# Two attention layers on one core: products cut in two and spread between the pieces of the heads, the first q by weight rows, the token sums' pool ahead of the prologue

## The chip, the cores and the metric

The kernel runs on one core of one Trainium2 chip. The metric is the device time of one execution in microseconds (us). Of the kernel before three runs are shown: 2143.07, 2144.46 and 2144.91 us; the median is 2144.46 us. One execution was also profiled; every view of a profile below is of that one execution.

Five engines work side by side, each through its own list of instructions: PE (TensorE, matrix products and transposes, with its weight loads shown apart as PEld), DVE (VectorE), ACT (ScalarE), POOL (GpSimd) and SP (SyncE, which here only issues DMAs). They wait for one another by semaphores.

## The reference

Two cross-attention layers, one after the other, over the same context. All arrays are float32. There are B = 8 batches, S = 100 queries, C = 640 channels in H = 20 heads of D = 32. The context has 77 text tokens, then 645 image tokens, of 1024 channels each.

```python
# layer 0 (x: 8 x 100 x 640; text = context[:, :77], ip = context[:, 77:])
q = x @ Wq.T
out = attend(q, text @ Wk.T, text @ Wv.T) + attend(q, ip @ Wk_ip.T, ip @ Wv_ip.T)
x1 = out @ Wo.T + bo + x
# layer 1, of x1, with weights of its own
q = x1 @ Wq
text_out = attend(q, text @ Wk, text @ Wv)
text_probs = softmax((q @ k_text.T) / sqrt(32))            # over all 640 channels
sem = ((text_probs @ text) @ ip.T) / sqrt(32)
ip_probs = softmax(scores_ip + 0.5 * sem) * mask           # mask: one number a query
out = (text_out + ip_probs @ v_ip) @ Wout + bout + x1
```

`attend` works head by head: softmax(q k / sqrt(32)) v. By far the most arithmetic is in the keys and values of the image tokens, 645 tokens by 1024 channels into 2 × 640 columns for each of 8 batches and 2 layers.

## The kernel before

**Units and steps.** A unit u is one batch in one layer: 16 of them (u = 8·layer + batch). Each is done in five steps p, one for each four heads (128 channels), so there are 80 steps n = 5u + p. The loop at the end (line 999 on) writes TensorE's order out by hand: `tc.manual_schedule` keeps PE in the order of the program text, and the other engines' orders are chosen by a scheduler and then fixed. One step holds

- `scores(u, p, 0)`: 4 matmuls of q by the first 512 keys into `sc` (line 782), then on DVE and ACT the row maxima and exponentials (lines 788 to 807);
- `transposes` of the step before, two tiles at a time, six in all (`pspt`, line 838): each is copied out of its bank into `pt` by DVE (line 845), every third by ACT (line 843);
- `scores(u, p, 1)`, the remaining 133 + 77 keys, and after it the small chain that joins the two parts (lines 811 to 828), with the last scaling of the probabilities on ACT (line 822) and DVE (lines 823 and 826);
- `values` of the step before (`pv`, line 860): probabilities by values, copied out by DVE (line 864).

**What fills the gaps.** Between those parts stand four calls `between(n, a, b, small)` (line 983). `small` holds the step's pieces: of a finished group of units the output projection in five pieces `out_piece` (`pso`, line 708, evicted by DVE with bias and residual at line 713), for layer 1 the next q in five pieces `q_piece` (`psq`, line 727, evicted by ACT at line 731), and three parts of `sem` (`psm`, lines 667 to 691). The rest is the production of keys and values for later units: `production()` (line 873) makes one list `todo` of tasks, each with a cost in us and a due step that `spread` works out so that each step gets about as much PE work as the others. `make(until)` runs the tasks that are due. After the pieces of a call one more task is taken ahead of its due time, when none was made in the call.

**Production.** Units 0 to 13 are made in pairs (`pair_tasks`, line 424), in five blocks of 128 tokens (133 in the last). A block begins with `begin`: it loads the next block's x, and has `token_sums` (line 182) form four sums of quarters of x on DVE and POOL. Then come `last_k` (`psk4`, line 453: 8 matmuls of 256 columns, for the last 128 key channels), for layer 1 two products of text by image (`psg`, line 465), and two series of seven products for the values (`psv`, line 475) and the other keys (`psk`, line 483): Strassen's scheme, in which the products of the series read the sums of x or of the weights. Product 1 (`psk_a`) reads x itself; the next, `psk_b`, is the first that needs a token sum. Units 14 and 15 are made singly (`single_tasks` and `last_tasks`), by `plain_product` (line 540, with its matmuls at line 544): 8 matmuls into one bank, then a copy.

**Memory.** [...] In the steps `sc` takes four, `ps_pt` two, which transposes, values and all pieces share in turn, and `ps_pj` two, for the products.

**The prologue** (lines 192 to 353) makes q of layer 0 and the text's keys and values of both layers. The first q: for each of five channel blocks c and two halves g of the batches, five matmuls over the rows k of Wq with 400 columns (4 batches), then an ACT copy (line 228) and stores by POOL (line 230). On SP the first loads are half of x, the five blocks of Wq, the other half of x, then the text and the text weights. `load_left` (line 311) loads eight weight blocks `wl` for the five image tokens beyond 640 (`left_v`, stored to `vl_d`). The prologue's memory, pool `first`, is given back at its end, and the pools of the steps, `sums` for the token sums among them (line 358), are laid out after that, over it.

Of the kernel before, what the change touches and what calls it, by code (L numbers as in the profile page):

```python
# [9 lines left out]
F32 = mybir.dt.float32  # L10
AF = mybir.ActivationFunctionType
# [3 lines left out]
P = 128  # L15
B = 8
# [27 lines left out]
def two_layer_xattn(  # L44
# [22 lines left out]
    cpool = ctx.enter_context(tc.tile_pool(name="ctx", bufs=2))  # L67
    dram = ctx.enter_context(tc.tile_pool(name="scratch", bufs=1, space=bass.MemoryType.DRAM))
# [61 lines left out]
    def product_ps(name):  # L130
        return pj[0].tile([P, 512], F32, tag="pj", name=name)
# [60 lines left out]
    with ExitStack() as es:  # L192
# [4 lines left out]
        nc.sync.dma_start(xt[:, :4], x_t[:, :4])  # L197
        for k in range(NC_):
            t = fp.tile([P, C], F32, tag="wq", name=f"wq0_{k}", bufs=NC_)
            nc.sync.dma_start(t, wq[0][k * P : (k + 1) * P, :])  # L200
            wq0.append(t)
        nc.sync.dma_start(xt[:, 4:], x_t[:, 4:])
# [13 lines left out]
        for c in range(NC_):  # L216
            t = fp.tile([P, B * S], F32, tag="q", name=f"q0_{c}", bufs=2)
            for g in range(2):
                ps = product_ps(f"psq_{c}_{g}")
                for k in range(NC_):  # L220
                    nc.tensor.matmul(
                        ps[:, : 4 * S],
                        lhsT=wq0[k][:, c * P : (c + 1) * P],
                        rhs=xt[:, 4 * g : 4 * g + 4, k, :],
                        start=(k == 0),
                        stop=(k == NC_ - 1),
                    )
                nc.scalar.activation(t[:, 4 * g * S : 4 * (g + 1) * S], ps[:, : 4 * S], AF.Copy, scale=SCALE)
            for g in range(B // 2):
                nc.gpsimd.dma_start(  # L230
                    q_d[0][g][:, :, c, :], t[:, 2 * g * S : 2 * (g + 1) * S].rearrange("p (b s) -> p b s", s=S)
                )

# [77 lines left out]
        def load_left(l):  # L311
            for k in range(NCC):
                wl[l, k] = fp.tile([P, C], F32, tag="wl", name=f"wl_{l}_{k}", bufs=NCC)
                nc.sync.dma_start(wl[l, k], wvi[l][k * P : (k + 1) * P, :])
# [43 lines left out]
    spool = ctx.enter_context(tc.tile_pool(name="sums", bufs=1))  # L358
# [65 lines left out]
    def pair_tasks(us):  # L424
# [12 lines left out]
        for j, (n0, n1) in enumerate(BLOCKS):  # L437
# [15 lines left out]
            def last_k(j=j, n=n, ko=ko):  # L453
                ps = product_ps(f"psk4_{us[0]}_{j}")
                for k in range(NCC):
                    nc.tensor.matmul(  # L456
                        ps[:, : 2 * n], lhsT=W["k", 4][:, k, :], rhs=xs[j][:, :, k, :n],
                        start=(k == 0), stop=(k == NCC - 1),
                    )
                nc.scalar.copy(ko[0][:, :, 4, :n], ps[:, : 2 * n].rearrange("p (i n) -> p i n", i=2))  # L460
# [52 lines left out]
            tasks.append((3.6, last_k))  # L513
# [26 lines left out]
    def plain_product(dst, n, lhs, rhs, name):  # L540
        ps = product_ps(name)
        m = dst.shape[0]
        for k in range(NCC):
            nc.tensor.matmul(ps[:m, :n], lhsT=lhs(k), rhs=rhs(k), start=(k == 0), stop=(k == NCC - 1))  # L544
        nc.scalar.copy(dst, ps[:m, :n])

    def wk_plain(c):
        def w(k):
            if c == 4:
                return W["k", 4][:, k]  # L550
            return W["k", f"b{k // HK + 1}{c // 2 + 1}"][:, k % HK, c % 2 * P : (c % 2 + 1) * P]

        return w

    def single_tasks(u):
        tasks, xs, text = [], {}, {}

        def begin():
            b = u % B
            for m in range(3):  # L560
                xs[m] = big_block(u, m)
            text[0] = one.tile([P, NCC, 2 * NT], F32, tag="textt", name=f"textt_{u}")
            nc.sync.dma_start(text[0][:, :, :NT], text_t.rearrange("k p n -> p k n")[:, :, b * NT : (b + 1) * NT])

        def k_one(c, m):
            n0, n1 = BIG[m]
            t = opool.tile([P, 256], F32, tag="ko", name=f"ko1_{u}_{c}_{m}")
            plain_product(t[:, : n1 - n0], n1 - n0, wk_plain(c), lambda k: xs[m][:, k, : n1 - n0], f"psk1_{u}_{c}_{m}")
            nc.gpsimd.dma_start(k_d[u][:, c, n0:n1], t[:, : n1 - n0])

        def v_one(j, h):
            t = opool.tile([P, HC], F32, tag="vo", name=f"vo1_{u}_{j}_{h}")
            at = j % 2 * P
            plain_product(
                t, HC, lambda k: xs[j // 2][:, k, at : at + P],
                lambda k: W["v", f"b{k // HK + 1}{h + 1}"][:, k % HK], f"psv1_{u}_{j}_{h}",
            )
            nc.gpsimd.dma_start(v_d[u][j * P : (j + 1) * P, h * HC : (h + 1) * HC], t)

        def text_one(m):  # L580
            n0, n1 = BIG[m]
            t = one.tile([NT, 2 * NX], F32, tag="gst", name=f"gst_{u}_{m}", bufs=2)
            plain_product(
                t[:, : n1 - n0], n1 - n0, lambda k: text[0][:, k, :NT], lambda k: xs[m][:, k, : n1 - n0],
                f"psg_{u}_{m}",
            )
            nc.gpsimd.dma_start(g_d[u % B][:, n0:n1], t[:, : n1 - n0])

        tasks.append((0.0, begin))
        for m in range(3):  # L590
            n = BIG[m][1] - BIG[m][0]
            tasks += [(0.0137 * n, lambda c=c, m=m: k_one(c, m)) for c in range(NC_)]
            tasks.append((0.0137 * n, lambda m=m: text_one(m)))
            tasks += [(4.3, lambda j=j, h=h: v_one(j, h)) for j in range(2 * m, min(2 * m + 2, NB)) for h in range(2)]
        return tasks

# [3 lines left out]
    def last_tasks():  # L600
# [17 lines left out]
        def text_one(m):  # L618
            n0, n1 = BIG[m]
            t = one.tile([NT, 2 * NX], F32, tag="gst", name=f"gst_{u}_{m}", bufs=2)  # L620
            plain_product(
                t[:, : n1 - n0], n1 - n0, lambda k: text[0][:, k, :NT], lambda k: xs[m][:, k, : n1 - n0],
                f"psg_{u}_{m}",
            )
            nc.gpsimd.dma_start(g_d[b][:, n0:n1], t[:, : n1 - n0])

        def k_one(c, m):
            n0, n1 = BIG[m]
            n = n1 - n0
            if c < 3:  # L630
                dst = opool.tile([P, 256], F32, tag="ko", name=f"ko1_{u}_{c}_{m}")[:, :n]
            else:
                if m == 0:
                    load_k(u, c)
                dst = ks[u, c][:, n0:n1]
            plain_product(dst, n, wk_plain(c), lambda k: xs[m][:, k, :n], f"psk1_{u}_{c}_{m}")
            if c < 3:
                nc.gpsimd.dma_start(k_d[u][:, c, n0:n1], dst)

        def v_one(c, j):  # L640
            if c < 3:
                dst = opool.tile([P, P], F32, tag="vo", name=f"vo1_{u}_{c}_{j}")
            else:
                if j == 0:
                    vs[u, c] = vpool.tile([P, NB, P], F32, tag="v", name=f"v_{u}_{c}")
                dst = vs[u, c][:, j, :]
            at = j % 2 * P
            plain_product(
                dst, P, lambda k: xs[j // 2][:, k, at : at + P], lambda k: wv[c][:, k // 2, k % 2], f"psv1_{u}_{c}_{j}"
            )  # L650
            if c < 3:
                nc.gpsimd.dma_start(v_d[u][j * P : (j + 1) * P, c * P : (c + 1) * P], dst)

        n = [b - a for a, b in BIG]
        return (
            [(0.0, begin)] + [(0.0137 * n[m], lambda m=m: text_one(m)) for m in range(3)],
            [[(0.0137 * n[m], lambda c=c, m=m: k_one(c, m)) for m in range(3)] for c in range(NC_)],
            [[(1.8, lambda c=c, j=j: v_one(c, j)) for j in range(NB)] for c in range(NC_)],
# [310 lines left out]
    with tc.manual_schedule(engines={mybir.EngineType.PE}):  # L969
# [8 lines left out]
        def make(until):  # L978
            while done[0] < len(todo) and todo[done[0]][1] < until:
                todo[done[0]][2]()  # L980
                done[0] += 1

        def between(n, a, b, small):


            before = done[0]
            for i, (_, f) in enumerate(small):
                make(n + a + (b - a) * (i + 1) / (len(small) + 1))
                f()
            make(n + b)  # L990
            while done[0] < len(todo) and todo[done[0]][1] < n + b + 0.4 and not any(
                t for t, _, _ in todo[before : done[0]]
            ):
                todo[done[0]][2]()
                done[0] += 1

# [85 lines left out]
```

## Time and profile before

| | |
|---|---|
| median of the runs shown | 2144.46 us |
| the profiled execution's own time | 2140.97 us |
| its span, first to last instruction | 2139.2 us |
| mean granted TensorE clock | 0.999 |
| PE busy | 2091.2 us (98%), 16670 instructions |
| PEld busy | 1677.7 us (78%) |
| DVE busy | 934.0 us (44%) |
| ACT busy | 864.5 us (40%) |
| POOL busy | 344.2 us (16%) |
| DMA | 241.99 MB, mean 113 GB/s |

The span is taken by the profiler, from the first to the last instruction; the execution's own time has some 2 us around it. A float32 matmul stands in the profile as two instructions ("passes"), each with a weight load of its own, so a product of 8 matmuls is "x16". Matmuls are pipelined: the next starts before one ends, so the pace is read from start to start and not from the length of one. A wait is put down to the instruction that ended it; "issue" means that the profile shows nothing that ended it.

### The profile page before, as it was taken

What the parts mean: (1) busy time and instruction counts of PE and PEld (TensorE: products, weight loads), DVE (VectorE), ACT (ScalarE), POOL (GpSimd) and SP (SyncE); (2) the same over time, 40 slices, a digit from 0 to 9 for tenths busy, and PEclk for the clock granted to TensorE, in tenths of its full rate; (3) what the DMA queues carried; (4) which work ended last, traced back from release to release, by engine and by line L of the source; (5) the groups of instructions that cost most, each with busy time, mean ns of one, the idle gap of its engine ahead of it and who ended that gap; (6) DMA issues with size and microseconds to landing.
All of it is one profiled execution on the core that took longest, in us unless ns stands there. A gap on an engine that the chain in (4) does not pass through costs nothing. (4 is left out here: it accounts for less than half of the span.)

```text
span 2139.2 us, 41528 instructions
## 1 busy us (share of the span) xinstructions
PE 2091.2 (98%) x16670; PEld 1677.7 (78%) x16670; DVE 934.0 (44%) x2380; ACT 864.5 (40%) x2859; POOL 344.2 (16%) x398
## 2 busy tenths in 40 slices
PE   8999999999999999999999999999999999999998
PEld 5676888787788887878878888887777887777887
DVE  1112122455454454454544444444444444454554
ACT  1001000345444444444344444444434445566665
POOL 5214112111010110102401111111111111111110
PEclk9999999999999999999999999999999999999999
DMA  9344223224234333535433333533333354334320
GB/s 344 106 134 163 79 78 102 85 78 124 77 113 136 95 104 104 150 90 165 120 116 114 110 100 93 154 85 99 83 113 99 95 158 128 119 96 122 106 81 7
DMA packets 264974, 241.99 MB, mean 113 GB/s; under 512 B 31466, under 2 KB 233722, under 8 KB 264782
## 3 DMA queue, kind: packets, MB, share of 16 engines
q1 hardware_dynamic: 245022, 171.97, 28.9%
q0 software_dynamic: 19760, 67.38, 9.4%
q8 instruction: 131, 2.15, 0.4%
q14 instruction: 61, 0.50, 0.1%
HBM read 171.68 MB, written 67.61 MB: 112 GB/s over the span
## 5 line engine op out<-in xcount | busy, mean ns | idle before, releaser
L845 DVE COPY pt<-pspt 128x400 f32<-128x400 f32 x320 | 175.6, 568 | 199.3 <-PE pspt L838 172.0
L799 ACT ACTIVATE p<-p,st 100x512 f32<-100x512 f32 (+1 forms) x320 | 176.4, 553 | 135.3 <-DVE st L795 135.3
L799 ACT ACTIVATE p<-sc,st 100x512 f32<-100x512 f32 (+1 forms) x320 | 165.2, 530 | 144.8 <-DVE st L788 144.3
L822 ACT ACTIVATE p<-p,st 100x512 f32<-100x512 f32 x320 | 204.8, 711 | 41.2 <-DVE st L818 39.6
L838 PE MATMUL pspt<-ident,p 100*128 100x100 f32 (+1 forms) x1920 | 209.0, 250 | 8.9 <-DVE pt L845 3.8
L838 PEld LDWEIGHTS pspt<-ident,p 100*128 100x128 f32 (+1 forms) x1920 | 186.5, 137 | 34.5 <-DVE res L713 5.8
L475 PE MATMUL psv_a<-wv,x 128*128 128x320 f32 x560 | 164.6, 437 | 1.5 <-ACT gst L470 1.3
L843 ACT COPY pt<-pspt 128x400 f32<-128x400 f32 (+1 forms) x160 | 78.2, 488 | 213.2 <-PE pspt L838 212.1
L475 PE MATMUL psv_d<-wv,s 128*128 128x320 f32 x560 | 163.5, 435 | 0.0
L795 DVE CUSTOM_DVE_ANT_0 p<-sc,sem 100x512 f32<-100x512 f32 (+1 forms) x320 | 138.8, 490 | 29.1 <-PE sc L782 29.1
L483 PEld LDWEIGHTS psk_a<-x,wk 128*128 128x128 f32 x1120 | 134.3, 193 | 11.9 <-DVE hs L864 3.9
L498 POOL DMA_DIRECT2D v_d<-vo x70 | 39.3, 561 | 632.1 <-DVE vo L172 471.9
L483 PE MATMUL psk_a<-x,wk 128*128 128x128 f32 (+1 forms) x1120 | 139.9, 278 | 1.0 <-ACT ko L148 1.0
L475 PEld LDWEIGHTS psv_a<-wv,x 128*128 128x128 f32 x560 | 102.9, 190 | 47.6 <-issue 5.7
L475 PEld LDWEIGHTS psv_d<-wv,s 128*128 128x128 f32 x560 | 104.4, 190 | 45.5 <-issue 3.1
L483 PE MATMUL psk_d<-s,wk 128*128 128x128 f32 (+1 forms) x1120 | 139.8, 278 | 0.0
L483 PEld LDWEIGHTS psk_d<-s,wk 128*128 128x128 f32 x1120 | 131.1, 191 | 10.2 <-issue 5.5
L782 PE MATMUL sc<-k,q 32*100 32x210 f32 (+1 forms) x1280 | 138.5, 502 | 0.3 <-ACT p L807 0.3
L788 DVE TENSOR_REDUCE st<-sc 100x4 f32<-100x2048 f32 x80 | 120.1, 1501 | 31.9 <-PE sc L782 31.8
L456 PE MATMUL psk<-x,wk 128*128 128x256 f32 (+1 forms) x560 | 128.5, 381 | 1.0 <-ACT vl L329 1.0
L510 POOL DMA_DIRECT2D k_d<-ko x70 | 58.5, 835 | 402.1 <-DVE ko L172 369.4
L456 PEld LDWEIGHTS psk<-x,wk 128*128 128x128 f32 x560 | 102.8, 188 | 18.8 <-DVE s L183 1.6
(177 smaller groups left out, 3393.0 us busy)
## 6 DMA issues: line engine op xcount, KB each, us to landing
x<-ip_t SPq DMA_DIRECT2D x56, 512.0 KB
k<-k_d SPq DMA_DIRECT2D x78, 322.5 KB
v<-v_d SPq DMA_DIRECT2D x78, 320.0 KB
v_d<-vo POOLq DMA_DIRECT2D x70, 320.0 KB, 2.5
k_d<-ko POOLq DMA_DIRECT2D x56, 320.0 KB, 6.8
o<-wo SPq DMA_DIRECT2D x40, 320.0 KB
x<-ip_t SPq DMA_DIRECT2D x16, 532.0 KB
q<-wq SPq DMA_DIRECT2D x20, 320.0 KB
```

The costliest lines, as they stand in the source:

```text
L456: nc.tensor.matmul(ps[:, : 2 * n], lhsT=W["k", 4][:, k, :], rhs=xs[j][:, :, k, :n], start=(k == 0), stop=(k == NCC - 1),)
L475: nc.tensor.matmul(ps[:, :HC], lhsT=sums[which][:, k, :P], rhs=W["v", WHICH[which]][:, k, :], start=(k == 0 and not go_on), stop=(k == HK ...
L483: nc.tensor.matmul(ps[:, r * n : (r + 1) * n], lhsT=W["k", WHICH[which]][:, k, r * P : (r + 1) * P], rhs=sums[which][:, k, :], start=(r == ...
L510: nc.gpsimd.dma_start(k_d[u][:, :, n0 : n0 + n], ko[0][:, h, :, :n])
L782: nc.tensor.matmul(sc[:S, i, : k1 - k0], lhsT=qs_[u][rows, c, :], rhs=ks[u, c][rows, k0:k1], start=True, stop=True)
L788: nc.vector.tensor_reduce(st[:, part, :], sc[:S, :, :n], AX.X, ALU.max, negate=True)
L795: nc.vector.tensor_tensor_reduce(out=img, in0=sc[:S, i, :n], in1=sems[u][:, k0 : k0 + n], scale=-1.0, scalar=3.0e38, op0=ALU.add, op1=ALU. ...
L799: nc.scalar.activation(p[:, i, k0 : k0 + n], img, AF.Exp, bias=st[:, part, i : i + 1], scale=sign, accum_out=st[:, 3 + part, i : i + 1],)
L822: nc.scalar.activation(p[:, i, :KA], p[:, i, :KA], AF.Copy, scale=mul[:, 0, i : i + 1])
L838: nc.tensor.transpose(ps[:rows, i * S : (i + 1) * S], pr[u, c][:, i, j * P : j * P + rows], ident[:S, :S])
L843: nc.scalar.copy(dst, src)
L845: nc.vector.tensor_copy(dst, src)
```

## The change

Four edits.

**The first q** goes through the batches in four pairs g. For each pair three banks are open at once, and the rows k of Wq are outermost: each row block meets all five channel blocks c before the next row is needed, with 200 columns (2 batches) a matmul. The loads of x are four instead of two, one a pair, the first of them ahead of Wq. A pair's q is stored by one DMA. Wq's five blocks and the eight `wl` blocks share one set of eight buffers, `wr`.

**The pool `sums`** is opened ahead of the prologue, so that it has memory of its own.

**Longer products in two tasks.** `last_k` is two tasks of 1.8 us, with the bank held from the first to the second. `plain_product` returns tasks, two halves where its cost is over 2.5 us.

**A product ahead of each piece.** `between` has a helper `apart`: before each piece of `small`, when no product was made since the last mark, tasks are taken from `todo` until one product is among them, as far as 0.4 step beyond the end of the call.

The function `text_one`, twice in the text before, stands once.

```diff
@@ pools
     cpool = ctx.enter_context(tc.tile_pool(name="ctx", bufs=2))
+    spool = ctx.enter_context(tc.tile_pool(name="sums", bufs=1))
     dram = ctx.enter_context(tc.tile_pool(name="scratch", bufs=1, space=bass.MemoryType.DRAM))
...
-    spool = ctx.enter_context(tc.tile_pool(name="sums", bufs=1))
     opool = ctx.enter_context(tc.tile_pool(name="made", bufs=2))
@@ the first q
-        nc.sync.dma_start(xt[:, :4], x_t[:, :4])
+        nc.sync.dma_start(xt[:, :2], x_t[:, :2])
         for k in range(NC_):
-            t = fp.tile([P, C], F32, tag="wq", name=f"wq0_{k}", bufs=NC_)
+            t = fp.tile([P, C], F32, tag="wr", name=f"wq0_{k}", bufs=NCC)
             nc.sync.dma_start(t, wq[0][k * P : (k + 1) * P, :])
             wq0.append(t)
-        nc.sync.dma_start(xt[:, 4:], x_t[:, 4:])
+        for g in range(1, B // 2):
+            nc.sync.dma_start(xt[:, 2 * g : 2 * g + 2], x_t[:, 2 * g : 2 * g + 2])
...
-        for c in range(NC_):
-            t = fp.tile([P, B * S], F32, tag="q", name=f"q0_{c}", bufs=2)
-            for g in range(2):
-                ps = product_ps(f"psq_{c}_{g}")
-                for k in range(NC_):
+        for g in range(B // 2):
+            t = fp.tile([P, 2, NC_, S], F32, tag="q", name=f"q0_{g}", bufs=2)
+            ps = [product_ps(f"psq_{g}_{i}") for i in range(3)]
+            for k in range(NC_):
+                for c in range(NC_):
+                    at = c % 2 * 2 * S
                     nc.tensor.matmul(
-                        ps[:, : 4 * S],
-                        lhsT=wq0[k][:, c * P : (c + 1) * P],
-                        rhs=xt[:, 4 * g : 4 * g + 4, k, :],
-                        start=(k == 0),
-                        stop=(k == NC_ - 1),
+                        ps[c // 2][:, at : at + 2 * S], lhsT=wq0[k][:, c * P : (c + 1) * P],
+                        rhs=xt[:, 2 * g : 2 * g + 2, k, :],
+                        start=(k == 0 and c % 2 == 0), stop=(k == NC_ - 1), skip_group_check=True,
                     )
...
+            nc.gpsimd.dma_start(q_d[0][g], t)
...
-                wl[l, k] = fp.tile([P, C], F32, tag="wl", name=f"wl_{l}_{k}", bufs=NCC)
+                wl[l, k] = fp.tile([P, C], F32, tag="wr", name=f"wl_{l}_{k}", bufs=NCC)
@@ longer products
-            def last_k(j=j, n=n, ko=ko):
-                ps = product_ps(f"psk4_{us[0]}_{j}")
-                for k in range(NCC):
+            def last_k(half, j=j, n=n, ko=ko, open_={}):
+                if half == 0:
+                    open_[j] = product_ps(f"psk4_{us[0]}_{j}")
+                ps = open_[j]
+                for k in range(HK * half, HK * (half + 1)):
...
-            tasks.append((3.6, last_k))
+            tasks += [(1.8, lambda h=h, f=last_k: f(h)) for h in range(2)]
...
-    def plain_product(dst, n, lhs, rhs, name):
-        ps = product_ps(name)
-        m = dst.shape[0]
-        for k in range(NCC):
-            nc.tensor.matmul(ps[:m, :n], lhsT=lhs(k), rhs=rhs(k), start=(k == 0), stop=(k == NCC - 1))
-        nc.scalar.copy(dst, ps[:m, :n])
+    def plain_product(time, make_dst, n, lhs, rhs, name, then=None):
+
+        parts = 2 if time > 2.5 else 1
+        open_ = {}
+
+        def part(i):
+            if i == 0:
+                open_["dst"], open_["ps"] = make_dst(), product_ps(name)
+            dst, ps = open_["dst"], open_["ps"]
+            m = dst.shape[0]
+            for k in range(NCC // parts * i, NCC // parts * (i + 1)):
+                nc.tensor.matmul(ps[:m, :n], lhsT=lhs(k), rhs=rhs(k), start=(k == 0), stop=(k == NCC - 1))
+            if i == parts - 1:
+                nc.scalar.copy(dst, ps[:m, :n])
+                if then:
+                    then(dst)
+
+        return [(time / parts, lambda i=i: part(i)) for i in range(parts)]
@@ a product ahead of each piece
+        mark = [0]
+
+        def apart(until):
+
+            while done[0] < len(todo) and todo[done[0]][1] < until and not any(
+                t for t, _, _ in todo[mark[0] : done[0]]
+            ):
+                todo[done[0]][2]()
+                done[0] += 1
+            mark[0] = done[0]
+
         def between(n, a, b, small):
-
-
-            before = done[0]
+
+            mark[0] = done[0]
             for i, (_, f) in enumerate(small):
                 make(n + a + (b - a) * (i + 1) / (len(small) + 1))
+                apart(n + b + 0.4)
                 f()
             make(n + b)
-            while done[0] < len(todo) and todo[done[0]][1] < n + b + 0.4 and not any(
-                t for t, _, _ in todo[before : done[0]]
-            ):
-                todo[done[0]][2]()
-                done[0] += 1
+            apart(n + b + 0.4)
```

## Prediction

> **What bounds the kernel.** I read the page's first two parts, then busy time by stretches, then TensorE's (PE's) waits, then the timeline where the longest ones fall. The stretches are the prologue with the first pair of images, the heads with enough products beside them, and the last heads with few products left:
>
> ```profile
> core 0: us, PE busy (x) PEld busy (x) DVE busy (x) ACT busy (x) POOL busy (x), PEclk, DMA share, GB/s
> 0.00:385.00 385.00, 373.79 (x1796) 275.68 (x1797) 80.49 (x121) 30.90 (x71) 102.04 (x99) 1.00 0.46 142
> 385.00:1730.00 1345.00, 1331.22 (x11226) 1090.08 (x11225) 652.56 (x1534) 596.06 (x1986) 197.87 (x223) 1.00 0.38 109
> 1730.00:2139.20 409.20, 386.15 (x3651) 311.90 (x3649) 200.96 (x725) 237.49 (x802) 44.34 (x77) 1.00 0.35 101
> ```
>
> TensorE is the bound, DVE and ACT at most six tenths busy. Idle TensorE is 385 − 373.79 = 11.2 us, then 13.8 us, then 23.05 us in the last 409 us alone: 48 of the 2139.2 us. No instruction of TensorE is removed by the change, so only these 48 us and losses of pace can be won. Who ended them (total, times, longest, all in us):
>
> ```profile
> PE psq L221 <- DMA wq<-wq: 6.9, 1, 6.9
> PE pso L708 <- DVE pt L845: 5.9, 12, 1.5
> PE pv L860 <- ACT pt L843: 4.8, 8, 0.8
> PE pspt L838 <- DVE pt L845: 3.8, 7, 0.9
> PE pspt L838 <- DVE res L713: 3.8, 9, 1.3
> PE psk_b L483 <- issue: 3.4, 1, 3.4
> PE psm L690 <- DVE pt L845: 2.9, 3, 1.0
> PE psq L727 <- DVE pt L845: 1.8, 5, 0.4
> ```
>
> One wait at the start, one of 3.4 us, and many small ones at the two banks of `ps_pt`: a piece (`pso`, `psq`, `psm`) or a transpose waits until DVE or ACT has copied out the tile before the last.
>
> **Part 1, the first q.** The first matmul starts at 6.85 us, when half of x (128 × 2000 × 4 B = 1.02 MB) and one weight block (0.33 MB) have landed. The change needs a quarter of x: 0.51 + 0.33 = 0.84 MB. By the DMA row of 0 to 60 us in 1.5 us slices (0, 187, 363, 371 GB/s: 0.28, 0.82, 1.38 MB at 3, 4.5 and 6 us), 1.35 MB were moved at 5.9 us and 0.84 MB at 4.5 us: **−1.3 us**. The next weight blocks come 0.8 us apart; [...] The wait for the second half of x goes (the second product took 16.17 − 12.58 = 3.59 instead of 3.36 us): −0.2.
>
> [...] here every load takes all 128 rows, and the change doubles them, 100 to 200 passes, by moving 200 columns instead of 400. [...] The row of this same shape:
>
> ```profile
> 644.77 3.65 PE L727 MATMUL psq<-res,q 128*128 128x200 f32 x20
> 648.26 0.94 PE L483 MATMUL psk_a<-x,wk 128*128 128x128 f32 x7
> ```
>
> 20 passes in 3.49 us, 174 ns each with their loads, against 200/400 × 336 = 168 ns: the loads are hidden. I follow the row: 200 × 0.170 + 0.1 (ten passes take 1.79 us, twenty 1.70 more) = 34.1 against 10 × 3.36 = 33.6: +0.5. The twenty q stores on POOL become four (0.72 us each by their row); TensorE waits for none of them. Sum **−1.0 us**, between +0.5 and −1.5. What follows has no idle TensorE up to 204 us, so the shift is kept. The shared buffers `wr` make the last five blocks of the first `load_left` wait on SP until q has read its rows, to about 41 us; behind them stand the two x blocks (39.5 us today) and the second layer's weights, which wait for TensorE anyway until 52.9 us. Cover is ample: those `wl` are used from 156.7 us.
>
> **Part 2, the pool of token sums.**
>
> ```profile
> 208.37 2.68 DVE L183 TENSOR_TENSOR s<-x 128x512 f32<-128x512 f32 x1 [0.62 <-DMA vl_d<-vl]
> 209.10 1.95 PE L483 MATMUL psk_a<-x,wk 128*128 128x128 f32 x16
> ...
> 213.75 1.72 POOL L185 TENSOR_TENSOR s<-x 128x512 f32<-128x512 f32 x1
> 214.41 2.17 PEld L483 LDWEIGHTS psk_b<-s,wkt 128*128 128x128 f32 x16 [3.56 <-issue]
> 214.44 2.43 PE L483 MATMUL psk_b<-s,wkt 128*128 128x128 f32 x16 [3.40 <-issue]
> ...
> 216.66 3.21 PE L483 MATMUL psk_a<-x,wk 128*128 128x128 f32 x16
> 219.60 1.87 PEld L483 LDWEIGHTS psk_c<-s,wkt 128*128 128x128 f32 x16
> 219.71 1.95 PE L483 MATMUL psk_c<-s,wkt 128*128 128x128 f32 x16
> ```
>
> The sums cannot start before the prologue's memory is free (the last store, `vl_d`), and `psk_b` waits for them. From `psk_a`, 1.79 us long elsewhere, `psk_b` should start at 210.89; it starts at 214.44: 3.55 us. After that gap the clock is halved: from 214.44 to 219.71 two products take 5.27 instead of 3.57: 1.70 us. With its pool outside the prologue's memory the sums are placed in DVE's and POOL's order some 150 us earlier, ahead of the first keys' copies (DVE 55.55 us today). They wait for x, issued near 42 us and about 1 MB long, some 3 us at 350 GB/s: done by 50. Next in line for `psk_b` is ACT's copy of `psk4`, at 209.4 + 0.4: before 210.89. The 0.96 us for `vl` stays. **−5.3 us**[...]: −3.6 to −5.3.
>
> **Part 3, the heads.** Here I count neighbours in the two programs' TensorE orders and take the loss of a neighbourhood from the timeline: start to next start, less the same group undisturbed (two transposes 0.69, `pv` 0.88 + 0.29).
>
> - Piece right behind two transposes: `pso` 12 → 2 times at 0.69 each, `psq` 5 → 0 at 0.53, `psm` 4 → 0 at 0.86: −6.9 − 2.7 − 3.4 = −13.0.
> - `pv` with no product ahead 5 → 2; the three that go (near 1805, 1897, 1946 us) lose 2.26 + 1.77 + 1.77 = 5.8: −5.8.
> - A `psm` whose ACT chain keeps a bank while transposes wait, six places, 4.9 us in sum, now with products on both sides: −4.0.
> - Near 1580 and 1330 us transposes right behind `pso` go: −2.1 and −0.7. Sum of gains −25.6.
> - Given back: transposes right behind `pso` or `psq` where a product stood before: about 12 new at 0.34: +4.1. One of them, near 1815 us, lands where DVE copies `pso` only behind the whole softmax chain. Such a case today:
>
> ```profile
> 1345.72 0.51 PE L838 MATMUL pspt<-ident,p 100*128 100x100 f32 x4
> 1347.53 0.54 PE L838 MATMUL pspt<-ident,p 100*82 100x100 f32 x4 [1.30 <-DVE res L713]
> ```
>
>  That is 1.8 between starts instead of 0.34, +1.3 beyond the above.
> - A half product (1.73 us) covers less than a whole one ahead of `pv`, as after 446.6 us, where 2.15 us left 0.44 idle: seven places, +2.4.
> - Each change of TensorE between kinds of work loses pace, 0 to 0.12 us, mean 0.05; there are 885 → 941 after the first scores: +2.8 (0 to +6.5).
>
> Heads: −25.6 + 10.6 = **−15.0 us**, of the some 45 us that they lose in all. The new waits have no row of their own in the trace: half of them gives −18, with free changes −20; twice the new waits and the dearest changes give −5.
>
> **Sum.** −1.0 − 5.3 − 15.0 = −21.3 us: 2140.97 → 2119.7 for the profiled execution (span 2139.2 plus 1.8 around it). That execution is 3.5 us under the median of the three runs, 2144.46, so I forecast **2123 us**. This case by itself: −28 to −12, 2116 to 2132. I give it 0.72.
>
> **Rivals.**
>
> *The heads give it back* (0.20, 2138 us). The waits are not cured but moved: DVE and ACT follow a fixed order, and products pulled forward leave the next steps short (about 15 instead of 22 us of TensorE near 670 and 900 us). Softmax from the second scores (655.65) to its last scaling (663.86) takes 8.2 us, so a short step can wait on it. For it: ACT is at 237 of the last 409 us, and the last heads' waits end on such chains. Against it: steps of 12.4 us near 1966 us have no wait today. Then only parts 1 and 2 remain: 2144.46 − 6.3 = 2138.
>
> *Split products cost more than they fill* (0.04, 2155 us; the slower side). A split product keeps one of the two `ps_pj` banks open across other work[...]. 69 products are split, 45 of them end up apart. The dearest change between two products in the trace, at 404.69 us, loses 0.39 us (2.54 between starts instead of 2.15); at 45 × 0.39 = 17.6 for cuts and no gain in the waits it is 2138 + 17 = 2155. It decides from 6.3/45 = 0.14 us a cut. Against it: the usual change costs 0.05.
>
> *It doesn't do what it says* (0.04, 2144 us). The early sums wait for x on DVE in front of the keys' copies; were x 6 us later than I have it, TensorE would stop near 55 us instead of at 211, and the heads give back the rest.
>
> A difference under 0.2% (4.3 us) cannot be told from none. Slower takes the second rival (0.04); within 0.2% takes the third, and a small part of the first (above 2140): 0.06; faster has 0.90. The range 2114 to 2135 takes in the forecast's bounds and the near part of the first rival.
>
> **What would show it.** First matmul near 5.5 us and the first text keys near 41.7 instead of 42.84; passes of 170 ns in q; no idle ahead of the first `psk_b`, no half clock after it; TensorE's idle time in the last 400 us down from 23 to about 12 us, `pso` and `psq` waits on `pt` nearly gone, waits of `pspt` on `res` and `qst` risen. Wrong would be: q passes over 180 ns, a new gap near 55 us, or heads that keep their 37 us of idle time under other names.

## The result, and the profile after

The changed kernel takes 2108.41 us (median of 6 runs, 2107.34 to 2110.06); the kernel before, run beside it, 2142.74 us (2141.55 to 2144.91). The ratio is 0.9839, with a 95% interval of 0.9826 to 0.9852. The forecast was 2123 us with a range of 2114 to 2135: the direction was right, the gain was larger than the range allowed. The profiled execution took 2109.68 us (span 2107.6) against 2140.97 (2139.2).

Busy time by stretches, cut at the first and near the last heads as before:

```profile
0.00:380.80 380.80, 374.45 (x1912) 292.37 (x1912) 78.80 (x122) 30.74 (x73) 90.21 (x84) 1.00 0.46 144
380.80:1725.00 1344.20, 1337.84 (x11268) 1096.01 (x11268) 658.40 (x1549) 599.34 (x2006) 198.16 (x223) 1.00 0.38 110
1725.00:2107.60 382.60, 372.52 (x3593) 302.95 (x3591) 198.43 (x709) 231.47 (x783) 43.55 (x75) 1.00 0.36 104
```

Length less the first number behind the comma is TensorE's idle time: 6.4, 6.4 and 10.1 us, where it was 11.2, 13.8 and 23.05. So 25 us of the 31.6 are idle time that went. The other 6 are time that the profile counts as busy: 1.7 of them are the halved clock after the gap near 214 us (3.42 us at half clock, last section); the rest was not broken down.

The longest waits of TensorE after (who waited for whom: total, times, longest, us):

```profile
PE psq L224 <- DMA wq<-wq: 5.4, 1, 5.4
PE pspt L857 <- DVE res L732: 4.3, 12, 1.3
PE pso L727 <- DMA o<-wo: 1.8, 2, 1.1
PE psg L472 <- ACT ko L467: 1.5, 2, 1.3
```

The start is 1.5 us shorter. Of the waits on `pt` that filled the list before (`pso` 5.9, `psq` 1.8, `psm` 2.9, `pv` 4.8, `pspt` 3.8) none is left above 0.5 us, and the 3.4 us ahead of `psk_b` have gone. What has risen, as forecast, is the wait of a transpose for `res`, that is for the piece right in front of it: 9 times to 12. New, and not forecast, is that `pso` waits twice for its weights (`wo`). Around the first `psk_b`, the timeline has no gap and no halved clock:

```profile
204.73 3.72 PE L461 MATMUL psk<-x,wk 128*128 128x256 f32 x16 [0.96 <-ACT vl L333]
208.29 1.95 PE L490 MATMUL psk_a<-x,wk 128*128 128x128 f32 x16
210.08 1.95 PE L490 MATMUL psk_b<-s,wkt 128*128 128x128 f32 x16
211.86 1.95 PE L490 MATMUL psk_a<-x,wk 128*128 128x128 f32 x16
213.65 1.95 PE L490 MATMUL psk_c<-s,wkt 128*128 128x128 f32 x16
```

The products start 1.79 us apart, with 1.95 us the length of one. `psk_c` starts at 213.65 instead of 219.71. The first scores of the heads start at 380.8 instead of 386.9 us: 6.1 us for parts 1 and 2. From there to the end it is 1726.8 instead of 1752.3 us: 25.5 us for the heads, where I had 15.0.

For the heads I take again the time from the start of a group of instructions (a tile's transposes, a product, a piece) to the start of the next, less the least that the same group needs in any of the kernels. Excess over 0.15 us is counted as a wait, the rest as loss of pace. No view shows these sums; they are added up from the starts in the traces, and forming the groups in another way moves a row by up to some 2 us, but none of the differences by more than 0.3:

| from the first scores on, us | before | after | forecast of the difference | measured |
|---|---|---|---|---|
| a piece (`pso`, `psq`, `psm`) right behind transposes | 14.0 | 2.3 | -13.0 | -11.7 |
| waits ahead of and inside `pv` | 12.2 | 2.2 | -5.8 + 2.4 | -10.0 |
| between transposes | 12.7 | 10.2 | -6.8 + 4.1 + 1.3 | -2.5 |
| all other waits | 6.7 | 6.0 | 0 | -0.7 |
| loss of pace in all changes of kind | 39.4 | 39.3 | +2.8 | 0.0 |

### The profile page after: what moved, and what is told of

The parts are those of the page before. It is cut to its first block, busy times and chain, and to the rows that moved or that the text cites. A ratio compares the mean times of both kernels' runs of the same rounds, so it can differ in the third digit from the quotient of the medians.

```text
span 2107.6 us, 41702 instructions
## 1 busy us (share of the span) xinstructions
PE 2084.8 (99%) x16770; PEld 1691.3 (80%) x16770; DVE 935.6 (44%) x2380; ACT 861.5 (41%) x2861; POOL 331.9 (16%) x382
## 5 line engine op out<-in xcount | busy, mean ns | idle before, releaser
L841 ACT ACTIVATE p<-p,st 100x512 f32<-100x512 f32 x320 | 204.8, 711 | 40.5 <-DVE st L837 39.4
L490 PEld LDWEIGHTS psk_a<-x,wk 128*128 128x128 f32 x1120 | 133.0, 191 | 10.1 <-DVE hs L883 3.1
L461 PEld LDWEIGHTS psk<-x,wk 128*128 128x128 f32 x560 | 102.2, 188 | 24.4 <-issue 7.1
```

Of the source, the lines that this page charges most:

```text
L461: nc.tensor.matmul(ps[:, : 2 * n], lhsT=W["k", 4][:, k, :], rhs=xs[j][:, :, k, :n], start=(k == 0), stop=(k == NCC - 1),)
L490: nc.tensor.matmul(ps[:, r * n : (r + 1) * n], lhsT=W["k", WHICH[which]][:, k, r * P : (r + 1) * P], rhs=sums[which][:, k, :], start=(r == ...
L841: nc.scalar.activation(p[:, i, :KA], p[:, i, :KA], AF.Copy, scale=mul[:, 0, i : i + 1])
```

## The experiments

All are edits of the changed kernel. Each ratio is against the kernel before, run on the same chip.

### Parts 1 and 2 alone

Both parts of the heads undone:

```diff
-        parts = 2 if time > 2.5 else 1
+        parts = 1
-            tasks += [(1.8, lambda h=h, f=last_k: f(h)) for h in range(2)]
+            tasks.append((3.6, lambda f=last_k: (f(0), f(1))))
...
-                apart(n + b + 0.4)
                 f()
```

> The changed kernel with the heads as before: products whole, no product ahead of each piece; the new first q and the early sums stay. If the two parts add up and the heads are a matter of their own, the first scores start at 380.8 us as in the changed kernel (386.9 before), and the rest of the program lasts 1752 us as before: span near 2133, ratio near 0.9972 (6.1 us). Rival: part of the heads' gain comes from the earlier start (other DMA timing, other order on DVE and ACT), so that 0.993 or less is seen with the heads as before.

Measured: 2134.80 us, ratio 0.9967 (0.9956 to 0.9978). First scores at 381.2 us, and from there 1751.5 us to the end. Waits of the heads: 45.1 us, before 45.6. The parts add up, and the earlier start does nothing for the heads.

### Each half of the heads' change alone

A product ahead of each piece, products whole (the first two edits above):

> The changed kernel with products whole again, but a product still ahead of each piece. In TensorE's order pieces right behind two transposes are 6 (21 before, 2 in the changed kernel), pv with no product ahead 6 (5 and 2), transposes right behind a piece 31 (14 and 22). By the rows of the trace before: -10 us for the pieces, +5 for the transposes, pv unchanged: the heads gain 5 of the 25.5 us, ratio near 0.995. Rival, that the product ahead of each piece is the whole of it and the split is incidental: 0.985 to 0.987.

Split products, a product only at the end of a part (the last edit above):

> The changed kernel with split products, but a product only at the end of a part as before. Pieces right behind two transposes stay 18 of 21, pv with no product ahead goes from 5 to 1. By the trace: -8 to -10 us for pv, -2.6 for psm; ratio near 0.992. Cuts that cost (my rival of 0.14 us or more each) would show here alone: 66 cuts at 0.14 us are +9 us, ratio 0.997 or above. Rival, that the product ahead of each piece is the whole of the gain: 0.997.

Measured: 0.9937 (0.9924 to 0.9949) and 0.9908 (0.9895 to 0.9922). Waits in the heads:

| us | heads as before | whole products | split alone | both (the change) |
|---|---|---|---|---|
| all waits | 45.1 | 41.0 | 32.2 | 20.7 |
| pieces behind transposes | 14.0 | 4.5 | 10.9 | 2.3 |
| between transposes | 12.7 | 16.7 | 14.2 | 10.2 |
| ahead of and inside `pv` | 12.2 | 12.4 | 1.4 | 2.2 |

Neither is the whole of it. The product ahead of each piece cures the pieces and does nothing for `pv`; the split cures `pv` and little of the pieces. The two alone save 4.1 and 12.9 us of waits, together 24.4: some 7 us come only from both. In time it is the same: 6.1 and 11.9 us alone, 26.4 together (2134.80 to 2128.73, 2122.95 and 2108.41 us). Where these waits are, TensorE's list for the last heads (from 1770 us) shows, first with whole products:

```profile
PE pspt L857 <- DVE pt L864: 4.9, 8, 1.2
PE pso L727 <- DMA o<-wo: 2.9, 3, 1.2
PE pv L879 <- DVE pt L864: 2.6, 5, 1.2
PE pv L879 <- ACT pt L862: 2.6, 4, 0.9
```

then split alone:

```profile
PE pspt L857 <- DVE pt L864: 5.0, 8, 0.7
PE pso L727 <- DVE pt L864: 3.9, 6, 1.5
```

With both, the two `pspt` rows of about 5 us are 0.3. In the last heads a step has few whole products: set ahead of the pieces, they are missing between the transposes and ahead of `pv`. Split alone, there are enough, but they stand at the ends of the parts. The run with whole products also lost clock: behind such waits its trace has two stretches of 3.4 us at half clock (near 1932 and 1952 us), by estimate 3.4 us lost (half of 6.8), in part counted as waits above; the changed kernel has none there. The forecast counted the neighbours of the final order and so has this in it; it is no cause of the error, but it is why half the change would have been worth much less than half.

### Part 1 undone

The first q as before, with x in halves, 400 columns a pass and twenty stores; the weight rows stay in the shared buffers.

> The changed kernel with the first q as before (half of x ahead of the weight blocks, 400 columns a pass, twenty stores). First matmul near 6.85 us instead of 5.39, text keys near 42.8 instead of 42.04, first scores near 381.6: +0.8 us, ratio against before 0.9843. Rival, that the twenty stores on POOL or the order of loads reach further: text keys on time but a new gap before 385 us, +2 us or more.

Measured: 0.9856 (0.9842 to 0.9869). First matmul at 6.57 us, text keys at 42.6, first scores at 381.4, 0.6 us later than in the changed kernel. The intervals of the two ratios overlap, so the time does not show the part; the trace does, and no new gap appears. The size of part 1 is taken apart below.

### Part 2 undone

The pool's line moved back behind the prologue:

```diff
-    spool = ctx.enter_context(tc.tile_pool(name="sums", bufs=1))
     dram = ctx.enter_context(tc.tile_pool(name="scratch", bufs=1, space=bass.MemoryType.DRAM))
...
     pj[0] = ctx.enter_context(tc.tile_pool(name="ps_pj", bufs=2, space=PSUM))
+    spool = ctx.enter_context(tc.tile_pool(name="sums", bufs=1))
```

> The changed kernel with the pool of the token sums back behind the prologue's memory, as before. Theory: the first sums wait again for the last store of the prologue, TensorE idles near 3.5 us ahead of the first psk_b, and where the clock is halved behind the gap it loses 1.7 more: first scores 5.26 us later (386.1), ratio 0.9863; runs without the halved clock 0.9855. Rival, that the early sums also cost something near 50 us (DVE and POOL busy with them ahead of the first keys' copies): then less than 3.5 us comes back.

Measured: 0.9868 (0.9853 to 0.9882), first scores at 387.3 us. The timeline around `psk_b`:

```profile
208.46 1.95 PE L490 MATMUL psk_a<-x,wk 128*128 128x128 f32 x16
213.73 3.75 PE L490 MATMUL psk_b<-s,wkt 128*128 128x128 f32 x16 [3.32 <-issue]
217.27 3.02 PE L490 MATMUL psk_a<-x,wk 128*128 128x128 f32 x16
220.13 1.95 PE L490 MATMUL psk_c<-s,wkt 128*128 128x128 f32 x16
```

From `psk_a` to `psk_b` it is 5.27 us instead of 1.79: the gap is back with 3.48. From `psk_b` to `psk_c` it is 6.40 us instead of 3.57: the low clock takes 2.83 us here, where it took 1.70 in the profile before. The stretches behind the gap show it in the column PEclk (0.50 is half clock), first before, then with the late sums, then the change:

```profile
213.50:216.00 2.50, 1.56 (x13) 1.59 (x14) 0.84 (x1) 0.00 (x0) 2.50 (x3) 0.98 1.01 337
216.00:217.00 1.00, 1.00 (x7) 1.00 (x6) 0.02 (x1) 0.00 (x0) 0.71 (x1) 0.50 1.15 317
```

```profile
213.50:216.00 2.50, 2.27 (x11) 2.31 (x12) 0.12 (x1) 0.00 (x0) 2.49 (x2) 0.50 1.06 336
```

```profile
213.50:216.00 2.50, 2.50 (x25) 2.50 (x25) 0.36 (x1) 0.37 (x1) 0.00 (x0) 1.00 1.09 331
```

Nothing is won near 50 us. The gap and its clock are the whole of part 2.

### Cut further

Long products in four, short ones in two:

```diff
-        parts = 2 if time > 2.5 else 1
+        parts = 4 if time > 2.5 else 2
...
-            tasks += [(1.8, lambda h=h, f=last_k: f(h)) for h in range(2)]
+            tasks += [(0.9, lambda h=h, f=last_k: f(h)) for h in range(4)]
```

> The changed kernel cut further: quarters of the long products (0.87 us each), halves of the 128-column ones. TensorE's order has one piece right behind two transposes (2), one pv with nothing ahead (2), 19 transposes right behind a piece (22), and 957 changes of kind (941). If cuts are free, as the whole sum of small losses says (38.5 us before, 37.3 after with 56 more changes), 1 to 2 us faster than the changed kernel, ratio 0.983. If each change costs 0.05 us, as my prediction charged, no better: 0.984. If a cut restarts something (0.14 us or more for each of some 150 more cuts): 0.993 or above.

Measured: 2116.54 us, 0.9882 (0.9866 to 0.9899). My expectation missed: it is some 8 us slower than the changed kernel (2108.41). The cuts are not the reason. The loss of pace is 39.9 us for 1488 groups, against 39.3 for 1461. It is waits, 28.6 instead of 20.7 us. Near 1768 us the timeline has, with quarters:

```profile
1768.34 0.51 PE L857 MATMUL pspt<-ident,p 100*128 100x100 f32 x4
1769.51 0.54 PE L857 MATMUL pspt<-ident,p 100*82 100x100 f32 x4 [0.67 <-DVE pt L864]
```

and the changed kernel at its place:

```profile
1765.52 0.71 PE L709 MATMUL psm<-g,tpt 77*100 77x323 f32 x2
1766.06 1.89 PE L558 MATMUL psk<-x,wk 128*128 128x256 f32 x8
1767.79 0.85 PE L857 MATMUL pspt<-ident,p 100*128 100x100 f32 x8
```

In both a `psm` piece holds one bank of `ps_pt` until its copy is done. Behind it stands a half product here (1.73 us from start to start), and the eight matmuls of transposes run through. With a quarter behind it (0.87 us) only the other bank is free, the second transpose waits until DVE has copied the first, and it comes 1.17 us after the first instead of 0.34. Seven such places, with 0.87 to 0.9 us behind the piece, lose 0.83 us each, 5.8 in all. Two things differ there: the transposes start 1.4 to 1.8 us after the piece's start instead of 2.3 to 2.7, and ACT's copy of the piece ends 2.7 to 3.0 us after it instead of 1.9 to 2.2. The shorter cover alone would have been too short in all seven, by 0.1 to 0.8 us; the later copy adds to it. Other waits come in at the products' own banks, as in `PE psv L558 <- ACT v L560: 1.1` and `PE psk L558 <- ACT ko L560: 1.0`. Counting what stands beside what had said "better"; how long it stands there, and when the copy comes, decide.

### Looking further ahead for a product

The product that keeps two pieces apart may be taken from 0.6 or 0.8 of a step ahead, in both calls:

```diff
-                apart(n + b + 0.4)
+                apart(n + b + 0.8)
```

> The changed kernel where the product that keeps two pieces apart may be pulled forward from 0.8 of a step ahead instead of 0.4. Transposes right behind a piece fall from 22 to 8 and pieces right behind transposes from 2 to 0: by 0.25 to 0.34 us each and 1.0 each, 4 to 6 us faster than the changed kernel, ratio 0.981 to 0.982. Rival, my forecast's first: products pulled forward leave the later steps short, and their pv waits: 0.985 or above, with waits of pv on pt back.

> The changed kernel with products pulled forward from 0.6 of a step ahead, between the 0.4 of the changed kernel and the 0.8 of the run before. Transposes right behind a piece 15 (22 at 0.4, 8 at 0.8), pieces right behind transposes 0. At 0.25 to 0.34 us each and 1.0 for each of the two pieces: 4 us faster than the changed kernel, ratio 0.982, between the two. Rival, that the gain at 0.8 came from elsewhere (other DMA times, an earlier start): no order among the three.

Whole products with 0.6 of a step:

> As the run with 0.6 of a step, but with products whole. In TensorE's order pv with no product ahead 4, psm right behind transposes 1, transposes right behind psm 10, double runs of transposes 7. If what stands beside each piece or pv alone decides, with whole products it stays near the run with whole products and 0.4 (0.9937), less 2 to 4 us: 0.992. Rival, that looking further replaces the split: 0.984 or below.

Measured: 0.9811 (0.9796 to 0.9825) with 0.8, and 0.9831 (0.9818 to 0.9845) with 0.6, between it and the 0.9839 (0.9826 to 0.9852) of the change. By time 0.8 is clear of the change and 0.6 is not; the order of the three is in the traces. Waits in the heads are 20.7 us with 0.4, 18.3 with 0.6 and 13.0 with 0.8, those between transposes 10.2, 8.0 and 5.8. Of the 9.5 us between the profiles of 0.4 and 0.8, 8.1 lie behind the first scores; the other 1.4 are a shorter stretch of slow passes at the start (1.4 us lost instead of 2.8, last section), with the same loads and passes of the first q in both. The rival, later steps left short, doesn't come: waits around `pv` are 2.2 us with 0.4, 3.7 with 0.6 and 1.9 with 0.8 (two of the short steps near 2015 us lose 0.3 and 0.4). With 0.8, `pso` no longer waits for `wo`, and the longest waits from 1770 us to the end read:

```profile
PE pspt L857 <- DVE res L732: 2.0, 5, 1.3
PE pspt L857 <- DVE pt L864: 0.9, 2, 0.6
PE psk L558 <- ACT k L560: 0.5, 1, 0.5
PE pv L879 <- ACT pt L862: 0.4, 2, 0.2
```

Whole products with 0.6 give 0.9915 (0.9901 to 0.9928), near the 0.992 expected: looking further doesn't replace the split. Its trace has three half-clock stretches of 3.4 us in the last heads. More than 0.8 of a step was not run.

### The first x in smaller parts

```diff
-        nc.sync.dma_start(xt[:, :2], x_t[:, :2])
         for k in range(NC_):
+            nc.sync.dma_start(xt[:, :2, k, :], x_t[:, :2, k, :])
```

> The changed kernel with the first x quarter loaded in five parts of 0.1 MB, each ahead of its own block of weight rows, so that the first matmul needs 0.43 MB instead of 0.84. By the load rate that the trace shows it starts near 3.8 us instead of 5.39; the later blocks come 1.2 us apart, under the time of ten passes. If all of it is kept, first scores 1.5 us earlier, ratio 0.983. Rival: [...] the third or fourth block is late: no gain or a loss of up to 1 us.

Together with 0.8 of a step:

> Products pulled forward from 0.8 of a step ahead together with the first x quarter loaded in five parts. First matmul near 4.5 us, heads as with 0.8: 0.9 us faster than with 0.8 alone, ratio 0.9807. Rival: the earlier start is lost in a longer stretch at low clock, as spread among the runs so far (1.4 to 3.1 us lost there): 0.981 or 0.982.

Measured: 0.9845 (0.9831 to 0.986) and 0.9811 (0.9798 to 0.9825). The first matmul starts at 4.52 us, 0.9 earlier and not the 1.6 expected; the first scores come 0.9 us earlier (379.9). That is too little to see in the time: no gain was shown. The fastest version that was run is therefore the change with 0.8 of a step, 2101.05 us (2101.49 with the smaller parts besides), faster than both kernels.

## Why the prediction was too small

**Bound and idle time: right.** TensorE bounds the kernel (busy 2084.8 of 2107.6 us after), and what could be won was its idle time and its pace. The 25.3 us of idle time that went are about half of the 48 named.

**Part 1: -1.0 forecast, -0.8 in the profile.** The first matmul starts 1.46 us earlier (forecast 1.3), the passes take 169.2 ns (170), which is 199 × 0.1692 = 33.7 us against 33.3 for the old shape. So the row decided rightly: a weight load stands in the trace with 190 ns, and with 100 loads more the passes still follow the columns, 169.2 ns for 200 against 336 ns for 400 before. The remaining difference is the slow start, which I had taken at the same cost in both, an estimate of mine that no trace showed. Before, the passes of 400 columns start 0.67 us apart up to 10.98 us and 0.336 us from then on, 2.1 us lost; after, those of 200 columns start 0.333 us apart up to 10.85 us, 2.8 us lost, and over the eleven profiles with this q it was 1.4 to 3.1 us (last section). No weight block after the first was waited for: ten of the slow passes take 3.3 us.

**Part 2: -5.3 forecast, -5.25 measured** (`psk_c` 6.06 earlier, less the 0.81 that `psk` already had from part 1). The early sums cost nothing, and undoing the part brings back the gap and the low clock.

**Part 3: -15.0 forecast, -25.5 measured.** Here it failed, in what I charged and left out around `pv` and for changes of kind, and not in the gains on pieces (-13.0 against -11.7; the two pieces that still stand behind transposes now wait 1.8 us for their weights and lose 1.2 us more than they did, which is most of the difference). By size:

- **`pv`: -3.4 forecast, -10.0 measured.** This was two errors. First, I counted as gains only the three places with no product ahead that go; they do (5.8). But seven more places had a short product or piece ahead and still waited, and they lost 4.8 us in sum; after the change places of that kind lose 0.6. Second, "a half product (1.73 us) covers less than a whole one ahead of `pv`", for which I charged 2.4, cost nothing: in the changed kernel seven `pv` have a half product of 1.8 us alone ahead, and none of them waits.

The reason can be read near 446.6 us, the place that I had taken the charge from. Before:

```profile
443.63 0.85 PE L838 MATMUL pspt<-ident,p 100*128 100x100 f32 x8
444.32 2.34 PE L475 MATMUL psv_a<-wv,x 128*128 128x320 f32 x8
444.85 2.56 ACT L822 ACTIVATE p<-p,st 100x512 f32<-100x512 f32 x4 [0.79 <-DVE st L818]
446.59 1.07 PE L860 MATMUL pv<-pt,v 128*32 128x100 f32 x40
447.56 0.48 ACT L843 COPY pt<-pspt 82x400 f32<-82x400 f32 x1
448.10 0.38 PE L860 MATMUL pv<-pt,vt 82*32 82x100 f32 x8 [0.44 <-ACT pt L843]
```

After, in the same step:

```profile
436.10 0.59 PE L857 MATMUL pspt<-ident,p 100*128 100x100 f32 x5
436.53 1.92 PE L461 MATMUL psk<-x,wk 128*128 128x256 f32 x8
437.87 0.48 ACT L862 COPY pt<-pspt 82x400 f32<-82x400 f32 x1
438.37 1.07 PE L879 MATMUL pv<-pt,v 128*32 128x100 f32 x40
438.83 2.56 ACT L841 ACTIVATE p<-p,st 100x512 f32<-100x512 f32 x4 [0.48 <-DVE st L837]
439.26 0.36 PE L879 MATMUL pv<-pt,vt 82*32 82x100 f32 x8
```

Before, a whole product of 3.5 us stood ahead of the last two transposes, so that they came late, and ACT's four scalings (2.56 us) went ahead of the copy of the sixth tile, which was done 3.56 us after the transposes. The wait was not due to a cover of 2.15 us being short by itself. After, half of that product has moved behind the transposes. They come earlier against the scalings, the copies follow at once (the sixth is done 1.66 us after the transposes), and the half product of 1.73 us is cover enough, the more so as the sixth tile is needed only when the first 40 matmuls of `pv` (0.88 us) are done. I had compared the cover with the lateness of that one place as if the lateness were fixed.

In all seven places the sixth copy stands right behind the scalings before. In five of them (446.6, 488.8, 1575, 2078 and 2094 us) it is ahead of them or well after them in the changed kernel, with a lateness of 0.5 to 1.7 us instead of 2.1 to 3.7; in the other two (1828 and 1965 us) the order stays and the work ahead of `pv` has grown by 1.7 to 2.2 us. The split alone brings the waits of `pv` from 12.2 to 1.4 us, so it is the split that does this. How much of it comes from each half having a due step of its own, and how much from the shorter product as such, no run separates.

- **Changes of kind: +2.8 forecast, 0.0 measured.** 56 more changes lost nothing in sum (39.4 and 39.3 us). The mean of 0.05 us for a change, which I had multiplied, is right for a mean and wrong for one more: products to pieces now lose 5.4 us where they lost 1.9, but what stands behind a piece lost 4.1 and loses 0.1. The loss belongs to a piece's neighbourhood, wherever in it the product is put.
- **Transposes: -1.4 forecast, -2.5 measured.** The new waits right behind `pso` and `psq` are there as charged: 13 new ones of 0.24 to 0.34 us and the one of 1.46 behind the softmax chain, near 1803 us, together 5.2 us for 5.4. The gains near 1580 and 1330 us (2.8) and around `psm` (4.1 for 4.0) came too. What I had not counted are two places with four tiles of transposes in a row, near 1870 and 1890 us, that lost 0.5 each and went.
- Other waits, forecast 0: -0.7.

The bounds I gave (half the new waits, or free changes: -18 to -20) moved one charge at a time; all charges of 10.6 us were against the same gain, two of them (2.4 and 2.8) were void, and the `pv` gain had no upper side at all. That made the range too narrow on the fast side. This accounts for the profiled execution, 2109.68 us for 2119.7. Another 4.8 us came from the last step of the sum: I set the new median 3.5 us above the new profile because the old one stood so, without asking why, and it stands 1.3 us below it. The last section has what the traces and clocks say of that.

**The rivals.** The heads do not give it back (37 us of idle time would have stayed, 16 are left). Split products do not cost: the run with quarters has many more cuts and the same pace (39.9 us lost for 1488 groups, 39.3 for 1461). The early sums are not late.

## What to carry to other kernels

Where one engine is full and its waits are short, list for each wait when the result that it needs is made, and not only how long the cover ahead of it is: cutting a long product in two moves work from ahead of the producer to behind it and helps twice. A cut may be free and still be too fine, if the piece no longer covers the wait at its place (1.73 us did, 0.87 did not, with the copy later as well). A mean cost per change of work is no price for one change more; look at what the neighbours give back.

## What was not expected of the hardware

The slow passes at the start did not take the same time in every profile. With the first matmul at 5.39 us (the change) and 5.32 us (0.8 of a step) the same q product took 36.5 and 35.1 us from its first pass to its last. Against 199 × 0.1692 us, the start lost 2.8 and 1.4 us; over the eleven profiles with this q it was 1.4 to 3.1. The stretches from 10 to 11 us of the two (TensorE's matmuls in the first brackets):

```profile
10.00:11.00 1.00, 1.00 (x5) 1.00 (x4) 0.00 (x0) 0.00 (x0) 0.00 (x0) 1.00 1.00 404
```

```profile
10.00:11.00 1.00, 1.00 (x8) 1.00 (x8) 0.00 (x0) 0.00 (x0) 0.00 (x0) 1.00 1.01 412
```

Five against eight recorded matmuls in the same us, and the clock column reads 1.00 in both. The column misleads here: each trace's first record of the clock, "full", comes at 10.96 us in the one and at 8.11 us in the other, and ahead of it the column shows 1.00 for want of a record. The passes show the pace: they start 0.33 us apart up to just these moments and 0.17 us apart from then on. Half of 10.96 - 5.39 us is 2.8, half of 8.11 - 5.32 us is 1.4, the two losses. So the start runs at half the later pace up to a moment that moved by 3.5 us among the eleven profiles (8.11 to 11.59 us), and a gain of 1 us in the first matmul's start is less than the 1.7 us between the smallest and the largest loss.

At the gap near 214 us, which ends at 214.44 us before and at 213.73 us with the late sums, the records read half clock from 215.88 to 219.30 us before, and from 212.69 to 219.52 us with the late sums: 3.42 and 6.83 us. Of the second, 5.79 us lie behind the gap's end; half of 3.42 and of 5.79 us, 1.7 and 2.9, are near the 1.70 and 2.83 us lost. The traces have seven half-clock stretches other than at the very start and end, and they last 3.4 or 6.8 us: these two, two with whole products and three with whole products and 0.6 of a step.

The five with whole products came without any long gap. With a product ahead of each piece, products whole:

```profile
1928.60 0.51 PE L857 MATMUL pspt<-ident,p 100*128 100x100 f32 x4
1930.27 0.54 PE L857 MATMUL pspt<-ident,p 100*82 100x100 f32 x4 [1.16 <-DVE pt L864]
1931.58 1.85 PE L879 MATMUL pv<-pt,v 128*32 128x100 f32 x40 [0.77 <-ACT tp L692]
```

```profile
1931.70:1935.10 3.40, 3.40 (x56) 2.13 (x54) 0.55 (x3) 0.20 (x1) 0.00 (x0) 0.50 0.12 30
```

The two waits are 1.16 and 0.77 us; in the 3.4 us ahead of each of the five TensorE was idle for 1.5 to 1.9 us in all, and no wait was over 1.2 us. So these five followed short waits that stand close together, with some 1.7 us lost each time (an estimate, half of 3.4). Such waits did not always bring it: in the kernel before, TensorE was idle for 1.91 of the 3.40 us from 1805.55 us and for 1.82 of those from 1961.68, and the clock read 1.00 there and in the 3.4 us behind each. What decides was not shown.

A lower mean clock also goes with the median of the old kernel standing above its profile. Of the 27 executions of the kernel before that ran beside the experiments, the 8 with a mean granted clock of 0.999 or 1.000 took 2140.05 to 2140.71 us, the 19 with 0.996 to 0.998 took 2142.04 to 2146.10; the profiled one (2140.97 us, 0.999) is like the 8. All six executions of the changed kernel have 0.999 or 1.000. So the medians differ by 34.3 us, the profiled executions by 31.3. Where the clock was lower in the 19 is not known, as those executions left no trace; with whole products the half-clock stretches stand behind waits in the last heads.
